# Reordering the first and last areas of an attention stage, its variance step, and the routing statistics of a mixture of experts

## The chip, the core and the metric

The kernel runs on one core of a Trainium2 chip. The metric is the device time of one execution in microseconds (us). The core has a tensor engine (PE, with its weight loads shown as PEld), a vector engine (DVE), a scalar engine (ACT), a general engine (POOL) and a queue engine for transfers (SP). Each executes its own instructions in the order in which the program gives them, and waits for the others by semaphores.

## The reference, cut to what matters

The input `x` has 2 images of 256 channels and 64 x 64 positions. Two layers follow each other; each adds a mixer and then a feed-forward part to `x`. The change touches the mixer of the first layer and the routing of the feed-forward part of the second.

```
x = x + area_attention(layernorm_over_channels(x))       # layer 0, mixer
t = t + lstm_like_recurrence(layernorm(t))               # layer 0, feed-forward
x = x + convs_and_mamba(layernorm_over_channels(x))      # layer 1, mixer
t = t + experts(layernorm(t))                            # layer 1, feed-forward
```

Area attention cuts the 4096 positions of each image into 4 areas of 1024. In every area and for each of 8 heads of 32 channels it computes `softmax(q k^T / sqrt(32)) v`, where q, k and v are products of the normalised input with weights, scaled and shifted per channel. A 5 x 5 convolution of v per channel (25 taps, over the borders of areas) is added, the sum is projected, and the result is added to `x`.

The experts' layer normalises 8192 tokens of 256 values, computes 8 logits for each, takes the two largest of the softmax, and adds the outputs of those two experts with their weights.

## The kernel before, in words

**Stages.** `body` calls `area_attention` (8 areas), then a recurrence and a second mixer, which together take the middle of the time, then `experts`. The last addition of attention to `x` (L345) is followed at once by the first transposes of the recurrence (L693), which read all of `x`. In `experts`, `route` calls `normalise`, then builds tables of indices, and `run_blocks` computes the experts' blocks.

**The attention loop.** Two groups of 4 heads (c = 0, 1) for each of 8 areas make 16 groups G, each with 16 steps t; one step handles 512 queries (n = t // 8) against 128 keys (m = t % 8). The loop at L555 does the following in each step, and the order of the instructions is the order written there (`manual_schedule`):

- `scores`: 4 small products that place the row maxima (L352), 4 that compute k q (L357), into two PSUM tiles of two banks; ACT takes the exponential of each (L364) into the tiles `ex`. There are three such PSUM tiles, `wide()`, for scores and maxima together, handed out in turn.
- `values` of the step before (L370, into `av_o`).
- small things at the time: `place` (L294 to L301) turns the negated maxima of a half group to rows, which ACT copies (L298) and SP sends to the tile `mx`.
- `maxima` for a coming group: 4 products into two `wide()` tiles (L270) and two reductions on DVE (L275). A group needs 16 of them before its own steps; a table (`AHEAD`) says which step computes which.
- on POOL one addition of two `ex` tiles (L577), from which the softmax sums are made. It is made to wait for the last product of this step's `maxima` and for the last marked DVE operation before it, so that it runs while DVE reduces.
- some taps of the convolution on DVE (L324; the first of each c is L313), as many as the table `TAPS` says.
- tables `MINE`, `SMALL`, `LATE`, `AROUND`, `LATE_AROUND` list further work by step: `query` and `key` (two products each at L166 and an ACT copy at L247), `v_half` (L166, L223), `v_tokens` (L239, L240), `mean` and `variance` (products with a constant matrix at L178, ACT copy at L179), `output` (L166, L339), `sums` (L370 into `po`, then L393, or the DVE chain L397 to L405), and on DVE `centre` (L187), `root` (transpose L199, power on POOL L202 and L203, transpose L206), `scale` (L212), `add_taps` (L332) and `residual` (L345). These products use one PSUM bank, `bank()`, of which there is one buffer.

The odd `ex` tiles have one buffer each, the even ones three: the exponentials of an odd step can only be written when POOL has added those of the odd step before.

**The start.** Before the loop, area 0 is normalised in two halves, by the generator `norm`, whose yields let other work be put between; then q and k of the first half are made and the first 8 maxima of group 0 run. A second set of tables with names in `_FIRST` holds for both groups of area 0: group 0 has two maxima in most of its steps, since its own second 8 and the 16 of group 1 are still missing.

**The end.** After the last step come the last sums, the addition of the taps (L332), the output products (L166) of both channel halves, and the two residuals (L345).

**normalise in experts.** For g = 0 to 15, PE turns 4 tiles of 128 tokens (L1730) and ACT copies them (L1731). Statistics are taken by DVE (L1736, one instruction for 128 values of 128 tokens) for groups 0 to 7 at g = 4 and 8 to 15 at g = 5; `root_in` (L1742 to L1747) and `root_out` (a square root on ACT at L1751, L1752, L1753) make the scale. The products with the centred gate weights (L1774, `gates`), a DVE copy (`take_gates`, L1782), transposes and a copy (`turn_gates`, L1788, L1789) give the logits in four parts; `choose` (L1830 to L1844, run once for each half) finds the two experts; `scale` (L1760 on POOL, L1764 on ACT) writes the normalised rows to DRAM by SP (L1767). After `choose` of the second half follow L1888 and a chain of DVE steps down to the indices (L1944), the fetch of the first weights (L1861) and 16 rounds that build the tables (L1954 to L1966), then the first gather of rows.

Of the kernel before, what the change touches and what calls it, by code (L numbers as in the profile page):

```python
# [18 lines left out]
P = 128  # L19
# [74 lines left out]
def area_attention(tc, sh, ap):  # L94
# [13 lines left out]
    with ExitStack() as ctx:  # L108
# [133 lines left out]
        def rows_of(wt, G, half, name, s, t):  # L242
            A, c = GROUPS[G]
            ps = bank()
            project(wt, c, columns(xns[A]), half, ps)
            out = p2.tile([P, 512], F32, name=f"{name}{half}")
            nc.scalar.activation(out, ps, AF.Identity, scale=s[:, c : c + 1], bias=t[:, c : c + 1])  # L247
            return out

        def query(G, half):  # L250
            if half == 0:
                nms[G] = p3.tile([P, NQ, GH, NM], F32, name="nm")
            qs[G, half] = rows_of(w["wq"], G, half, "q", s_qk, t_qk)

        def key(G, half):
            ks[G, half] = rows_of(w["wk"], G, half, "k", s_qk[:, 2:4], t_qk[:, 2:4])
# [152 lines left out]
        with ExitStack() as own:  # L409
# [10 lines left out]
            def norm(at, half):  # L420
# [6 lines left out]
                root(0, 0, at)  # L427
                root(0, 1, at)
                yield
# [7 lines left out]
            next(second)  # L437
            for _ in first:
                pass
            query(0, 0)  # L440
            key(0, 0)
# [4 lines left out]
            next(second)  # L446
            maxima(0, 2)
            key(0, 1)
            maxima(0, 3)
# [9 lines left out]
            for at, works in enumerate([  # L459
                [(0, 0), (0, 1)], [(1, 0)], [(1, 1)], [],  # L460
            ]):
                maxima(0, at + 4)
                for c, half in works:
                    v_half(0, c, half)
            join(0, 0, nc.vector)
            place(0, 0)
            for half in range(2):
                v_tokens(0, 0, half)
# [11 lines left out]
                2: [(0, v_tokens, 1, 0)], 3: [(0, v_tokens, 1, 1)], 4: [(-1, output, 0, 0)],  # L480
                6: [(1, variance, 0)], 7: [(1, variance, 1)], 8: [(-1, output, 0, 1)],
# [11 lines left out]
                3: [(1, square, 1)], 7: [(1, root, 0)],  # L493
# [5 lines left out]
        FIRST = [  # L499
            {  # L500
                0: [(0, query, 1)], 1: [(1, query, 0)], 2: [(1, key, 0)], 3: [(1, key, 1)],
                4: [(1, query, 1)], 14: [(2, query, 0)], 15: [(2, key, 0)],
            },
            {0: [(1, key, 1)], 2: [(1, query, 1)], 11: [(2, query, 0)], 12: [(2, key, 0)], 15: [(2, key, 1)]},
        ]
        SMALL_FIRST = [{5: [(0, place, 1)], 13: [(1, place, 0)]}, SMALL]
        LATE_FIRST = [{4: [(0, join, 1)], 9: [(1, join, 0)], 13: [(1, join, 1)]}, LATE]
        AROUND_FIRST = [
            {
                6: [(1, mean, 0)], 7: [(1, mean, 1)], 8: [(0, v_tokens, 1, 0)], 10: [(1, variance, 0)],  # L510
                11: [(1, variance, 1)], 12: [(0, v_tokens, 1, 1)],
            },
            {
                1: [(1, v_half, 0, 0)], 3: [(1, v_half, 1, 0)], 4: [(1, v_half, 0, 1)], 6: [(1, v_half, 1, 1)],
                7: [(1, v_tokens, 0, 0)], 8: [(1, v_tokens, 0, 1)], 10: [(2, mean, 0)], 14: [(2, mean, 1)],
            },
        ]
        LATE_AROUND_FIRST = [
            {
                7: [(1, centre, 0)], 8: [(1, centre, 1), (1, square, 0)], 9: [(1, square, 1)],  # L520
                11: [(1, root, 0)], 12: [(1, root, 1), (1, scale, 0)], 13: [(1, scale, 1)],
            },
            LATE_AROUND[1],
        ]
# [4 lines left out]
        AHEAD_FIRST = [{}, {**AHEAD, 0: [(1, 0), (1, 1)], 1: [(1, 2), (1, 3)]}]  # L529
        for t in range(1, 14):  # L530
            AHEAD_FIRST[0][t] = [order.pop(0) for _ in range(2 if t < 12 else 1)]

# [5 lines left out]
            [3] + [0] * 11 + [2, 2, 4, 4],  # L538
            [1, 1, 3, 2, 2, 2, 3, 2, 2, 2, 2, 3, 3, 2, 3, 2],
# [15 lines left out]
        for g in range(16 * len(GROUPS)):  # L555
# [3 lines left out]
            new = A == 0  # L559
# [5 lines left out]
            works(G, t, SMALL_FIRST[c] if new else SMALL, {})  # L565

            mm, before = None, latest[0]
            for k, at in (AHEAD_FIRST[c] if new else AHEAD).get(t, ()):
# [12 lines left out]
            for _ in range((TAPS_FIRST if new else TAPS)[c][t]):  # L581
                next(conv, None)
            works(G, t, FIRST[c] if new else MINE, (AROUND_FIRST if new else AROUND)[c])
            if g in due:
                sums(*due.pop(g))
            works(G, t, LATE_FIRST[c] if new else LATE, (LATE_AROUND_FIRST if new else LATE_AROUND)[c])
# [6 lines left out]
            else:  # L593
                pairs = (pairs if m % 4 else []) + [exs]
        nc.gpsimd.tensor_tensor(pairs[-1][1], pairs[-1][1], odd, ALU.add)
        values(*pending)
        for g in sorted(due):
            sums(*due[g])
        last = len(AREAS) - 1
        add_taps(last, 1)  # L600
        for co in range(2):
            for half in range(2):
                output(last, co, half)
            residual(last, co)
# [1014 lines left out]
def experts(tc, sh, ap, out, half, left):  # L1619
# [19 lines left out]
    with ExitStack() as ctx:  # L1639
# [64 lines left out]
        def normalise(p2, logits, halves):  # L1704


            with ExitStack() as own:
# [89 lines left out]
                for g in range(TILES // K):  # L1797
# [9 lines left out]
                    if g == 5:  # L1807
                        for i in range(8, TILES // K):
                            measure(i)
                        root_in()  # L1810
                    if 4 < g < 12 and g % 4 == 2:
                        turn_gates(*waiting)
                    if g == 10:
# [449 lines left out]
```

## Time and profile before

| | us |
|---|---|
| median of 3 runs (3035.07 to 3035.3) | 3035.14 |
| the profiled execution itself | 3031.56 |
| its span, first to last instruction | 3029.7 |
| attention's first step begins (first L352) | 69.85 |
| second group of area 0 begins | 184.2 |
| area 1 begins | 290.2 |
| areas 2 to 6 begin | 467.9, 643.8, 818.7, 994.1, 1170.9 |
| last step's exponentials (L364) begin | 1492.1 |
| last residual of attention ends | 1530.97 |
| first transposes of the experts' normalise | 2324.17 |
| first table step (L1954) | 2384.96 |
| first gather of rows | 2424.6 |

Over the span PE is busy for 90%, DVE 72%, ACT 44%, POOL 45%. A timeline row reads: start, duration, engine, line, operation, output and input with shapes, count, and in brackets the idle time before it and what ended that. A wait row reads: who waited for whom, total, times, longest. A window row gives the busy time of each engine in a stretch, with the number of instructions, and the clock that PE was granted as a share of full speed.

### The profile page before, as it was taken

How to read it: one execution, taken by the hardware profiler on the slowest of the kernel's cores; microseconds unless marked ns; L12 is line 12 of the kernel's file. 1: busy time of each engine (PE TensorE's matmuls, PEld its weight loads, DVE VectorE, ACT ScalarE, POOL GpSimd, SP SyncE). 2: the span in 40 equal slices, each digit the busy share in tenths (PEclk: the TensorE clock that was granted, in tenths of full speed). 3: DMA queues.
4: the chain of work that ended last, by engine and by line, in shares of the span. 5: the costliest groups of instructions: out<-in, count | busy, mean ns of one | idle time of the engine just before them, and what ended most of it. 6: DMA issues, size and time to landing. Idle time of an engine off the chain costs nothing. (4 is left out here: it accounts for less than half of the span.)

```text
span 3029.7 us, 45443 instructions
## 1 busy us (share of the span) xinstructions
PE 2738.2 (90%) x17798; PEld 1519.2 (50%) x17798; DVE 2181.1 (72%) x3224; ACT 1347.7 (44%) x2417; POOL 1358.4 (45%) x1037
## 2 busy tenths in 40 slices
PE   6989999999999999998789999978887589999994
PEld 2222232332323233222179999963444478888882
DVE  4689999999989999898956676679988812222115
ACT  2334454554544454444444455557653822222223
POOL 1354545544454554545623000028773156666651
PEclk8999999999999999999889999989999789999995
DMA  3000000000000000000024000005552446666658
GB/s 126 1 1 1 1 1 1 1 1 1 1 1 1 1 1 1 2 1 1 5 87 161 2 1 1 2 12 153 146 145 64 159 164 228 227 226 227 227 189 337
DMA packets 58658, 220.33 MB, mean 73 GB/s; under 512 B 14440, under 2 KB 15344, under 8 KB 48704
## 3 DMA queue, kind: packets, MB, share of 16 engines
q0 software_dynamic: 25440, 125.24, 11.6%
q1 hardware_dynamic: 31760, 87.82, 9.0%
q10 hardware_dynamic: 1232, 4.25, 0.4%
q8 instruction: 142, 2.33, 0.3%
q14 instruction: 84, 0.69, 0.1%
HBM read 173.30 MB, written 43.58 MB: 72 GB/s over the span
## 5 line engine op out<-in xcount | busy, mean ns | idle before, releaser
L577 POOL TENSOR_TENSOR ex<-ex,ex 128x1024 f32<-128x1024 f32 x255 | 614.5, 2412 | 645.3 <-PE ps L270 287.5
L275 DVE TENSOR_REDUCE nm<-ps 128x2 f32<-128x1024 f32 x512 | 601.0, 1218 | 102.4 <-PE ps L270 101.6
L364 ACT ACTIVATE ex<-ps 128x1024 f32<-128x1024 f32 x512 | 497.9, 1022 | 308.2 <-PE ps L357 269.3
L324 DVE SCALAR_TENSOR_TENSOR acc<-vh,w_pe,acc 128x1008 f32<-128x1008 f32 (+7 forms) x384 | 553.0, 1442 | 7.1
L270 PE MATMUL ps<-k,q 32*128 32x512 f32 x2048 | 347.7, 644 | 13.1 <-DVE nm L275 13.1
L2007 DVE COPY xt<-px 128x512 f32<-128x512 f32 x68 | 47.0, 691 | 397.7 <-PE px L2005 397.7
L2019 ACT ACTIVATE act<-ph,wt 128x256 f32<-128x256 f32 x272 | 128.8, 474 | 396.0 <-PE ph L2017 391.9
L2017 PE MATMUL ph<-xt,wt 128*128 128x256 f32 x1088 | 293.2, 393 | 3.3 <-ACT act L2019 1.7
L357 PE MATMUL ps<-q,k 32*128 32x512 f32 x2048 | 285.0, 607 | 0.0
L370 PE MATMUL av_o<-ex,vt 128*32 128x512 f32 x2048 | 278.0, 609 | 4.8 <-ACT ex L364 4.6
L2027 PE MATMUL py<-wt,act 128*128 128x256 f32 x1088 | 279.6, 380 | 0.0
L270 PEld LDWEIGHTS ps<-k,q 32*128 32x128 f32 x2048 | 123.1, 184 | 216.1 <-issue 75.0
L2017 PEld LDWEIGHTS ph<-xt,wt 128*128 128x128 f32 x1088 | 191.6, 192 | 66.4 <-DVE xt L2007 23.4
L774 PE MATMUL z<-xs,u 128*128 128x128 f32 x1872 | 222.2, 275 | 0.4 <-ACT xs L754 0.4
L774 PEld LDWEIGHTS z<-xs,u 128*128 128x128 f32 x1872 | 215.7, 192 | 0.6 <-ACT xs L754 0.6
L2027 PEld LDWEIGHTS py<-wt,act 128*128 128x128 f32 x1088 | 202.2, 191 | 25.0
L798 ACT ACTIVATE t<-z,bias 128x128 f32<-128x128 f32 x468 | 136.3, 361 | 144.5 <-PE z L786 144.4
L2042 POOL DMA_INDIRECT results<-y,ri x136 | 138.0, 1015 | 139.4 <-DVE y L2035 98.3
L786 PE MATMUL z<-xs,v 128*128 128x128 f32 x1512 | 180.1, 275 | 0.1
L786 PEld LDWEIGHTS z<-xs,v 128*128 128x128 f32 x1512 | 174.3, 192 | 0.7 <-DVE xs L805 0.7
L1508 POOL TENSOR_TENSOR cs<-hs,cs 128x1024 f32<-128x1024 f32 x63 | 148.7, 2363 | 54.1 <-DVE hs L1501 32.7
L370 PE MATMUL po<-ex,ones 128*32 128x512 f32 x1024 | 136.6, 638 | 37.0 <-ACT rows L298 25.7
(408 smaller groups left out, 3809.9 us busy)
## 6 DMA issues: line engine op xcount, KB each, us to landing
cs<-c_rows SPq DMA_DIRECT2D x128, 256.0 KB
y<-results SPq DMA_DIRECT2D x32, 512.0 KB
x<-xrows SPq DMA_DIRECT2D x8, 1024.0 KB
rows<-xt SPq DMA_DIRECT2D x16, 512.0 KB
out_x<-res POOLq DMA_DIRECT2D x15, 512.0 KB, 7.1
xrows<-xn SPq DMA_DIRECT2D x24, 256.0 KB
x<-in_x SPq DMA_DIRECT2D x4, 1024.0 KB
x<-in_x ACTq DMA_DIRECT2D x4, 1024.0 KB
```

The costliest lines, as they stand in the source:

```text
L270: mm = nc.tensor.matmul(tiles[h // 2][:, h % 2], qs[G, i // HM][head(h), i % HM * P : (i % HM + 1) * P], ks[G, n][head(h)], start=True, st ...
L275: nc.vector.tensor_reduce(nms[G][:, n, 2 * j : 2 * j + 2, i], tiles[j], AX.X, ALU.max, negate=True)
L324: mark(nc.vector.scalar_tensor_tensor(part, vh[:, c, 2 + r0 + dy : 2 + r1 + dy, w0 + dx : w1 + dx], w_pe[:, c, k : k + 1], part, ALU.mult, ...
L357: nc.tensor.matmul(tiles[h // 2][:, h % 2], k[head(h), m % HM * P : (m % HM + 1) * P], qs[G, n][head(h)], start=False, stop=True, tile_pos ...
L364: nc.scalar.activation(exs[i], tiles[i], AF.Exp, scale=HD**-0.5)
L370: nc.tensor.matmul(to[head(h)], lhs, exs[h // 2][:, h % 2], start=first, stop=last, tile_position=(0, HD * h))
L577: add = nc.gpsimd.tensor_tensor(pair[0], *pair, ALU.add)
L774: nc.tensor.matmul(z[c][:, g, :m], u[:, k, c, g], xt[:, k], start=g == GATES[0] and k == 0, stop=False, skip_group_check=True,)
L786: nc.tensor.matmul(z[c][:, g, :m], v[:, k, c, g], h[:, k], start=False, stop=k == 1, skip_group_check=True,)
L1508: nc.gpsimd.tensor_tensor(now["c", n], hs, now["c", n], ALU.mult)
L2017: nc.tensor.matmul(ph[:, hc], wt[:, at : at + P], xt[:, c], start=c == 0, stop=c == 1)
L2027: nc.tensor.matmul(py[:, j], act[:, hc, j * P : j * P + P], wt[:, at : at + C], start=hc == 0, stop=hc == NH - 1,)
```

## The change

The diff has two parts.

In attention:

- `query` and `key` can take a PSUM place from outside. Before the loop, q and k of the first half use `wide()` tiles instead of the single bank; q of the second half of group 0 and q and k of group 1 are made before the loop as well (they were steps 0 to 2 of group 0).
- The two `mean` steps of area 1 are put in before the first half of area 0 is scaled (they were steps 6 and 7 of group 0).
- In `norm`, the yield between the two halves of `root` is moved, so that two maxima can stand between the power on POOL and the DVE transpose that waits for it. The four `v_half` and the two `v_tokens` are spread between the maxima, and the join and place of the first maxima come after them.
- The tables `_FIRST` hold for group 0 alone; group 1 of area 0 uses the ordinary tables, but keeps its own numbers of taps. Group 0 has two maxima in steps 0 to 9 and one after; no taps before step 10.
- In the ordinary tables, `variance` moves from steps 6 and 7 to 4 and 6, the output that was in step 4 to step 7, and the first half of `root` from step 7 to step 6; the second half stays in step 8.
- After the loop the end is done by halves of 512 positions: add the taps of the half, two output products into one `wide()` tile, ACT copies, residuals; the last sums come between the halves.

In `normalise`: statistics for groups 8 to 11 are taken at g = 5, those for 12 to 15 and `root_in` at g = 9; `root_out` and the first `choose` move from g = 10 to 13; all 16 `scale` steps come after the loop, where 5 of them stood in it.

```diff
-            query(0, 0)
-            key(0, 0)
+            for half in range(2):
+                mean(1, half)
+            for _ in first:
+                pass
+            query(0, 0, wide()[:, 0])
+            key(0, 0, wide()[:, 0])
             next(second)
             maxima(0, 0)
             next(second)
             maxima(0, 1)
-            next(second)
             maxima(0, 2)
+            for _ in second:
+                pass
+            maxima(0, 3)
             key(0, 1)
-            maxima(0, 3)
...
+            for at in range(4):
                 maxima(0, at + 4)
+                v_half(0, *divmod(at, 2))
+            for half in range(2):
+                v_tokens(0, 0, half)
+            query(0, 1, wide()[:, 0])
             join(0, 0, nc.vector)
             place(0, 0)
+            query(1, 0, wide()[:, 0])
+            key(1, 0, wide()[:, 0])
...
-                2: [(0, v_tokens, 1, 0)], 3: [(0, v_tokens, 1, 1)], 4: [(-1, output, 0, 0)],
-                6: [(1, variance, 0)], 7: [(1, variance, 1)], 8: [(-1, output, 0, 1)],
+                2: [(0, v_tokens, 1, 0)], 3: [(0, v_tokens, 1, 1)], 4: [(1, variance, 0)],
+                6: [(1, variance, 1)], 7: [(-1, output, 0, 0)], 8: [(-1, output, 0, 1)],
...
-                3: [(1, square, 1)], 7: [(1, root, 0)],
+                3: [(1, square, 1)], 6: [(1, root, 0)],
...
+        FIRST = {
+            0: [(1, key, 1)], 1: [(1, query, 1)], 11: [(2, query, 0)], 12: [(2, key, 0)], 15: [(2, key, 1)],
+        }
...
+        AHEAD_FIRST = dict(AHEAD)
+        for t in range(14):
+            AHEAD_FIRST[t] = [order.pop(0) for _ in range(2 if t < 10 else 1)]
...
         TAPS_FIRST = [
-            [3] + [0] * 11 + [2, 2, 4, 4],
-            [1, 1, 3, 2, 2, 2, 3, 2, 2, 2, 2, 3, 3, 2, 3, 2],
+            [0] * 10 + [1, 2, 3, 2, 3, 2],
+            [2, 0, 2, 2, 3, 3, 3, 2, 2, 0, 3, 3, 3, 3, 3, 3],
         ]
...
+        for half, at in enumerate(HALVES):
+            if half == 1:
+                for g in sorted(due):
+                    sums(*due[g])
+            y = ys[last, 1][:, at]
+            nc.vector.tensor_tensor(y, y, acc[:, at], ALU.add)
+            ps = wide()
+            for co in range(2):
+                project(w["wpr"], co, lambda k: ys[last, k], half, ps[:, co])
...
+                to = area(last)[:, co, at]
+                nc.vector.tensor_tensor(to, to, o, ALU.add)
...
-                    if g == 5:
-                        for i in range(8, TILES // K):
+                    if g in (5, 9):
+                        for i in range(g + 3, g + 7):
                             measure(i)
+                    if g == 9:
                         root_in()
                     if 4 < g < 12 and g % 4 == 2:
                         turn_gates(*waiting)
-                    if g == 10:
+                    if g == 13:
                         root_out()
                         halves[0]()
-                    if g > 10:
-                        scale(g - 11)
                 last = gates(3)
                 turn_gates(*take_gates(*waiting))
                 turn_gates(*take_gates(*last))
-                for g in range(5, TILES // K):
+                for g in range(TILES // K):
                     scale(g)
```

## The prediction

> **What bounds the kernel now.** I first read the busy times by stage, cut at step starts (the first L352 of a step), then the timeline of each stage that the diff touches, then the waits. The middle stages and the experts' blocks are untouched and only start earlier or later: the first transposes after attention begin 0.5 us after its last residual, and the first gather follows 16 table rounds. So the change is worth what it takes off attention's end and off the start of the tables.
>
> Stages (stretch; length; then busy us of PE, PEld, DVE, ACT, POOL; clock):
>
> ```profile
> 71.60:184.20 112.60, 106.30 (x607) 32.96 (x607) 77.46 (x70) 42.21 (x50) 44.78 (x29) 0.96 0.00 1
> 184.20:290.20 106.00, 95.85 (x583) 29.66 (x582) 96.23 (x84) 43.57 (x52) 43.59 (x29) 0.94 0.00 1
> 467.90:643.80 175.90, 170.05 (x1125) 53.40 (x1124) 164.87 (x149) 86.00 (x102) 89.34 (x55) 0.99 0.01 1
> ...
> 1489.80:1531.50 41.70, 23.41 (x66) 6.50 (x62) 24.64 (x31) 6.89 (x10) 8.03 (x6) 0.67 0.03 7
> ```
>
> In an ordinary area (third row) PE is busy 97% and DVE 94%. Area 0 (first two rows) takes 218.6 us where an ordinary one takes 176: its first group is PE's (DVE idles 35 us), its second DVE's. The last 41.7 us are neither's, a chain of waits.
>
> The start:
>
> ```profile
> 22.08 3.75 PE L166 MATMUL po<-xn,wq 128*128 128x512 f32 x4 [6.35 <-issue]
> ...
> 26.70 3.69 PE L166 MATMUL po<-xn,wk 128*128 128x512 f32 x4 [0.87 <-ACT q L247]
> ...
> 31.26 1.98 PE L178 MATMUL po<-sq,mean_w 128*128 128x512 f32 x4 [0.87 <-ACT k L247]
> ...
> 40.82 0.71 DVE L206 STREAM_TRANSPOSE ln_r<-root 128x512 f32<-128x512 f32 x1 [3.49 <-POOL root L203]
> ...
> 73.89 1.94 ACT L364 ACTIVATE ex<-ps 128x1024 f32<-128x1024 f32 x2 [3.35 <-PE ps L357]
> ```
>
> One projection takes 3.7 us after a PE idle of 6.35 us and 1.98 us later; the single bank puts an ACT copy between q and k; DVE stands 3.49 us for POOL's power with maxima behind it.
>
> Step 8 to 9 of an ordinary area (area 2):
>
> ```profile
> 513.23 5.46 POOL L203 TENSOR_TENSOR root<-root,minus_half 128x32 f32<-128x32 f32 x1
> ...
> 518.65 2.34 POOL L577 TENSOR_TENSOR ex<-ex,ex 128x1024 f32<-128x1024 f32 x1
> 518.72 1.25 DVE L206 STREAM_TRANSPOSE ln_r<-root 128x1024 f32<-128x1024 f32 x1 [3.21 <-POOL root L203]
> ...
> 521.03 1.02 ACT L364 ACTIVATE ex<-ps 128x1024 f32<-128x1024 f32 x1 [3.50 <-POOL ex L577]
> ...
> 522.25 3.31 PE L370 MATMUL po<-ex,ones 128*32 128x512 f32 x16 [3.54 <-ACT rows L298]
> ```
>
> Power, POOL's addition, the exponential that needs its buffer, the rows copy behind it on ACT, PE's sums behind that: step 9 takes 10.4 us (515.14 to 525.50) where its neighbours take 5.35.
>
> The end of attention, and the routing:
>
> ```profile
> 1515.97 3.78 PE L166 MATMUL po<-y,wpr 128*128 128x512 f32 x4 [0.87 <-ACT o L339]
> ...
> 1529.75 1.22 DVE L345 TENSOR_TENSOR x<-x,o 128x1024 f32<-128x1024 f32 x1 [7.93 <-ACT o L339]
> ```
>
> ```profile
> 2346.04 0.42 DVE L1747 TENSOR_REDUCE var<-away 128x64 f32<-128x256 f32 x1
> ...
> 2363.29 0.29 DVE L1789 COPY logits<-by_token 128x128 f32<-128x128 f32 x1 [7.05 <-PE by_token L1788]
> ...
> 2365.31 0.57 DVE L1830 TENSOR_TENSOR pr<-logits,inv 128x256 f32<-128x256 f32 x1
> ```
>
> Every output product runs at the slow rate with an ACT copy in between. In the routing DVE idles 7.05 us before the third part of the logits, since the last turns wait on ACT behind scales.
>
> **What the Trainium skill says.** "TensorE: Matmul & The Clock Gate", "What's actually happening": PE runs at half clock by default and at full clock after about 3.4 us of sustained work. The trace agrees: 3.7 against 1.98 us for the same four products. "SBUF — State Buffer", "Who interferes with whom": a DVE instruction with two SBUF inputs and a POOL instruction that reads SBUF exclude each other for a whole instruction. The trace agrees: the L212 pair beside the addition at 518.65 takes 2.08 us for one operation and 1.21 us elsewhere; a tap and an addition issued back to back take turns, 3.3 us a pair (POOL's 16.01 us for 5 additions at 1469.47), against 1.3 for a tap alone.
>
> **Part by part.**
>
> *Start.* The two means of area 1 fill PE from 16.4 to 21.0 (1.98 each plus a 0.58 copy; the x of area 1 has landed by 12.3 us, by its transfer's packets), so the clock stays up: q 22.05 to 24.0, and k at once after it from its own PSUM tile, done on ACT at 26.8 instead of 31.2. First maxima at 27.9 instead of 33.2. Power hidden behind two maxima (4.7 us of DVE against 3.5): k of the second half at ACT by 40.9 instead of 48.8. Then the four rounds of maxima and v at the 2.98 us pace of the old trace, from 42.1 to 53.1; tokens 2.5, q of the second half 2.0, place at 57.9. The rows go out at 58.75; the old trace has 4.6 us from the rows copy to the last L352 (67.02 to 71.62), hence 63.35, and q and k of group 1 (4 us) lie inside that. The loop is entered some 8.3 us earlier with 8 us of PE projections and the means (4 us) already done.
>
> *Group 0.* A step with two maxima and a projection took 7.6 us (100.56 to 108.17), without projection 5.7, with tokens 6.3. New steps 0 to 9: 6.1, 7.6, 6.3, 6.3, 7.6, 7.6, 7.6, 5.7, 5.7, 7.6, sum 68.1; DVE's root, two scales and sums pile up in 7 to 9, +1.5: step 10 at 133. DVE then has, of the 173.7 us that both groups had (77.5 + 96.2), plus 3 for the taps that ran ahead of the loop, minus 4 for taps that stood for POOL around 184, 172.7; some 55 of it done by then (20 maxima at 2.27, 45; centre, transposes, scale, sums, 10). The rest, 117.7 us, is more than PE's (30 for steps 10 to 15, 82 after), so DVE is the bound at its ordinary 96 to 97%: 121.5 us. Area 1 begins at 254.5 to 261 against 290.2; with a little more DVE debt handed on I take **31 us** saved, bounds 22 and 36.
>
> *Variance and root one step earlier* (six areas). POOL's order is now root, addition 7, addition 8. In area 2's times: DVE ends the two taps of step 6 at 508.0, transposes to 509.2; power ends at 515.1, addition 7 at 517.4. The transpose after it no longer waits. But the scale reaches DVE at 517.3, just before addition 8 can start; if it takes its turn first, addition 8 ends at 521.0, as now, and nothing is gained; if POOL wins, it ends at 519.8 and the step is 1.2 us shorter, with a warmer clock 2. Behind DVE's earlier transpose, one reduction is late by 0.65 us, which the later stall covers. I take 0.5 per area, **3 us**; bounds -4 (0.65 uncovered) and +14 (six times 2.3). The output moved to step 7 costs PE the same two products.
>
> *End.* Taps end at 1505.6 and are unchanged. add_taps 1.22, half-add 0.68; two products 3.8 and 2.8 (slow, then warming) to 1513.5; sums 2.0, the DVE chain 3.1 and add 0.7 to 1519.3; remaining products 3.0, copy 0.78, residual 0.68: 1523.8 to 1524.5 against 1530.97. **6.5 us**, bounds 3 (all slow) and 8. The setup of the next stage (1.21 us wait for bc_rest on DVE) falls in gaps.
>
> *Routing.* Two counts of statistics: 16 at 0.193 after the first gates, then DVE waits for the second gates (PE 2340.45) and takes 30 more: to 2347.0. root_in 2.7: 2349.7, that is 3.3 us later than 2346.46. Root and first choose 2.9 + 6.3: 2358.9. Two rounds of copy, transpose, copy: 3.5: second choose at 2362.4 instead of 2365.31. **2.5 us** after a slow-clock allowance; bounds 0 and 4. The 16 scales now lie after the turns: ACT 16 x 1.49 from 2353.5 to 2377.4, before 2378.4, so the exponents behind them are no later; the SP row writes end 40 us before the first gather.
>
> Sum: 31 + 3 + 6.5 + 2.5 = 43. The profiled execution's 3031.56 becomes 2988.6; the median of the runs stands 3.6 us above it, so 2992.
>
> **Rivals.** *A, area 0 gives less*: PE cools between the sparse maxima at 31 to 37 us, and the three-tap steps hold PE through the shared PSUM tiles, as at 184 to 205 (PE idle 8 us). For: DVE has no slack there. Against: additions are tied to reductions. Then 20 instead of 31 and nothing from the root: 3006. *B, POOL wins the race* in the six areas: 11 us more, 2981. *C, slower*: the root in step 6 puts POOL's additions off the reductions, and they stay off, so that taps take turns with them: 2.0 us for each tap met. Area 0's second group (37 taps) and six areas meet them; from about 22 taps on the gain of 43 is eaten, at 4 per area and 8 in area 0 (32 taps, 64 us) it is 3056. Against: by step 10 POOL has 3 us of slack in each step. *D, nothing*: the last PE wait just moves to the area's other stalls, 3033.
>
> **Numbers.** Likeliest case 0.62, own range 2984 to 3002; A 0.18, B 0.15, C 0.03, D 0.02. The bounds of the terms added are -21 and -62 (3014, 2973); all ends do not fall together, and 2978 to 3010 leaves under 2 in 10 out. Faster 0.95, within 0.2% (6 us, about what can be told from no change) 0.02, slower 0.03.
>
> **What would show it.** Start: the first L364 near 64.5, q and k of the first half at 1.98 us. Area 0: area 1 begins near 258, DVE over 95% busy in its second group. Root: no wait of L206 for L203, yet ACT's wait for POOL's L577 stays once in each area. End: last L345 18.5 us after the last tap. Routing: L1747 later, L1954 earlier by 2 to 3 us. I am wrong if area 1 begins after 270, or if step 9 still costs as much while something else in an ordinary area grows.

## The result, and the profile after

The changed kernel takes 3003.18 us (median of 3 runs, 3001.11 to 3006.58) against 3035.14: a ratio of 0.990, 95% interval 0.9886 to 0.9914. It is faster by 32 us; forecast were 43 (2992, range 2978 to 3010). The time lies inside that range, but 1 us outside the range given for the likeliest case (2984 to 3002), and nearer to the 3006 of rival A than to 2992.

The profiled execution of after is the one of 3003.18 us, span 3001.4, so between the two profiles the gain is 28.3 us. The rest of the 32 is that the profiled execution of before lay 3.6 us under its median and that of after on it. Read by stage, from marks in the two timelines (the forecast of the first row is the prediction's for the entry of the loop; its own mark for the first exponential, 64.5 us, would be 9.4):

| stage ends at | before | after | gain in the stage | forecast |
|---|---|---|---|---|
| first exponential (L364) | 73.89 | 65.60 | 8.3 | 8.3 |
| area 1 begins (first L352) | 290.2 | 266.1 | 15.8 | 22.7 |
| last tap of attention ends | 1505.67 | 1477.27 | 4.3 | 3 |
| first transposes of the recurrence | 1531.51 | 1505.57 | -2.5 | 6.5 |
| first transposes of normalise | 2324.17 | 2298.12 | 0.1 | 0 |
| second choose begins | 2365.31 | 2336.85 | 2.4 | 2.5 |
| first gather of rows | 2424.58 | 2396.35 | -0.2 | 0 |
| end of the span | 3029.7 | 3001.4 | 0.1 | 0 |

Two stages carry nearly the whole error: area 0 gave 7 us less, and the end lost 2.5 where 6.5 were to be gained.

The stages again as windows (stretch; length; busy us of PE, PEld, DVE, ACT, POOL; clock), cut at the same places as before: group 0 and group 1 of area 0, and the end.

```profile
64.30:175.20 110.90, 103.74 (x607) 31.84 (x607) 84.87 (x76) 41.31 (x48) 43.79 (x31) 0.94 0.00 1
175.20:266.10 90.90, 84.87 (x561) 26.13 (x561) 88.17 (x80) 41.43 (x49) 40.78 (x26) 0.98 0.00 1
...
1461.40:1505.60 44.20, 19.40 (x71) 5.59 (x71) 26.25 (x33) 7.79 (x10) 10.56 (x15) 0.73 0.05 12
```

Group 1 is DVE's to 97%, as forecast, and 15 us shorter. Group 0 is only 1.7 us shorter than the 112.6 of before. Three projections (6 us of PE) and two means (4 us) left it, but PE's busy time fell only from 106.3 to 103.7 us: one projection (k of area 1's first group), a `v_half` and two more rounds of maxima came in, and part of the rest ran at the lower clock (0.94 against 0.96). The last stretch, which was to shrink, is longer.

The start in the timeline of after:

```profile
22.23 1.98 PE L166 MATMUL ps<-xn,wq 128*128 128x512 f32 x4 [0.99 <-DVE xn L212]
24.05 1.88 PE L166 MATMUL ps<-xn,wk 128*128 128x512 f32 x4
...
36.15 0.69 DVE L206 STREAM_TRANSPOSE ln_r<-root 128x512 f32<-128x512 f32 x1
...
65.60 1.94 ACT L364 ACTIVATE ex<-ps 128x1024 f32<-128x1024 f32 x2 [1.99 <-PE ps L357]
```

q and k follow each other at 1.98 and 1.88 us, no idle time stands before the transpose L206, and the first exponential begins 1.1 us after the forecast 64.5.

Step 8 to 9 of area 2 (POOL's additions are L564 here):

```profile
488.50 5.46 POOL L203 TENSOR_TENSOR root<-root,minus_half 128x32 f32<-128x32 f32 x1
...
493.93 7.96 POOL L564 TENSOR_TENSOR ex<-ex,ex 128x1024 f32<-128x1024 f32 x3
...
494.79 1.24 DVE L206 STREAM_TRANSPOSE ln_r<-root 128x1024 f32<-128x1024 f32 x1
...
496.06 1.31 DVE L212 TENSOR_TENSOR xn<-xn,ln_r 128x1024 f32<-128x1024 f32 x1
...
499.60 1.02 ACT L364 ACTIVATE ex<-ps 128x1024 f32<-128x1024 f32 x1 [2.26 <-POOL ex L564]
...
500.82 2.49 PE L370 MATMUL po<-ex,ones 128*32 128x512 f32 x16 [2.29 <-ACT rows L298]
```

The scale in before, where POOL's addition had begun first:

```profile
520.00 2.08 DVE L212 TENSOR_TENSOR xn<-xn,ln_r 128x1024 f32<-128x1024 f32 x1
```

DVE no longer waits for the power; ACT still waits for POOL's addition, 2.26 us instead of 3.50, and PE behind it 2.29 instead of 3.54. That is what was to be seen. In the race between DVE's scale and POOL's second addition DVE has the first turn, in all six areas: the scale takes 1.31 us instead of 2.08, and the addition 3.32 instead of 2.34. Counted from the start of step 7 that addition ends only 0.3 us sooner than in before (16.3 against 16.6 us in area 2).

The end:

```profile
1492.79 3.78 PE L166 MATMUL ps<-y,wpr 128*128 128x512 f32 x4 [0.87 <-ACT o_last L597]
...
1497.42 0.69 DVE L601 TENSOR_TENSOR x<-x,o_last 128x512 f32<-128x512 f32 x1 [3.96 <-ACT o_last L597]
...
1498.41 0.65 POOL L1119 DMA_DIRECT2D bc_rest<-in_b_conv  x1 [27.97 <-DVE bc_parts L628]
...
1504.42 0.76 PE L1116 MATMUL w_dt<-w_dtp,w_xdt 4*128 4x128 f32 x2 [7.85 <-DMA w_dtp<-in_w_dtp]
...
1505.57 4.75 PE L690 MATMUL turned<-ident,x 128*128 128x128 f32 x24 [0.38 <-DVE w_dt L1117]
```

The last residual (L601) ends 20.8 us after the last tap, against 25.3 before. But the transfers of the next stage's setup are only issued after it, and its product w_dt waits for them on PE, ahead of the first transposes. In before they were issued at 1505.8 to 1506.6, 24 to 25 us before the last residual ended, and the transposes followed that residual by 0.5 us. Now they follow it by 7.5. Before:

```profile
1505.81 0.36 SPq L1107 DMA_DIRECT2D taps<-in_c_rows  x1
...
1506.27 0.65 POOL L1122 DMA_DIRECT2D bc_rest<-in_b_conv  x1 [7.42 <-issue]
```

The routing, on DVE:

```profile
2323.41 0.42 DVE L1744 TENSOR_REDUCE var<-away 128x64 f32<-128x256 f32 x1
...
2336.52 0.29 DVE L1786 COPY logits<-by_token 128x128 f32<-128x128 f32 x1 [1.27 <-PE by_token L1785]
2336.85 0.42 DVE L1826 TENSOR_TENSOR pr<-logits,inv 128x256 f32<-128x256 f32 x1
```

Counted from normalise's first transposes the variance is ready 3.4 us later (forecast 3.3) and the second choose starts 2.4 us sooner (2.5); the idle 7.05 us is gone.

### The profile page after: what moved, and what is told of

It is laid out like the page before. It is cut to its first block, busy times and chain, and to the rows that moved or that the text cites. A ratio compares the mean times of both kernels' runs of the same rounds, so it can differ in the third digit from the quotient of the medians.

```text
span 3001.4 us, 45442 instructions
## 1 busy us (share of the span) xinstructions
PE 2724.7 (91%) x17798; PEld 1512.9 (50%) x17798; DVE 2173.2 (72%) x3227; ACT 1348.5 (45%) x2417; POOL 1358.1 (45%) x1037
## 5 line engine op out<-in xcount | busy, mean ns | idle before, releaser
L564 POOL TENSOR_TENSOR ex<-ex,ex 128x1024 f32<-128x1024 f32 x255 | 617.3, 2425 | 615.1 <-PE ps L270 248.9
L364 ACT ACTIVATE ex<-ps 128x1024 f32<-128x1024 f32 x512 | 498.0, 1022 | 318.2 <-PE ps L357 285.5
L370 PE MATMUL av_o<-ex,vt 128*32 128x512 f32 x2048 | 280.8, 615 | 4.8 <-ACT ex L364 4.6
L352 PE MATMUL ps<-mx,ones_b 3*128 3x512 bf16 x1024 | 132.4, 386 | 37.2 <-DVE nm L275 35.0
```

Source lines behind the costliest of these rows:

```text
L364: nc.scalar.activation(exs[i], tiles[i], AF.Exp, scale=HD**-0.5)
L370: nc.tensor.matmul(to[head(h)], lhs, exs[h // 2][:, h % 2], start=first, stop=last, tile_position=(0, HD * h))
L564: add = nc.gpsimd.tensor_tensor(pair[0], *pair, ALU.add)
```

## The experiments

In the experiments the executions of one kernel, before included, spread over 4 to 17 us, much of it in stages that nobody edited (from the first transposes of the recurrence to those of normalise: 789.5 to 800.7 us in the 14 profiles). So small effects are read from the profile of each kernel, by stage, and the times stand beside them. Each stage is then one execution of one kernel; where several kernels share a stage, their spread is given. Ratios are to the kernel before on the same chip; they lie up to 0.0012 from the quotients of the medians beside them.

| kernel | median us | before beside it | ratio, 95% interval |
|---|---|---|---|
| routing alone | 3037.02 | 3038.72 | 0.9993 (0.9984 to 1.0001) |
| end alone | 3041.28 | 3038.72 | 1.0003 (0.9992 to 1.0014) |
| after, o_last elsewhere | 3006.94 | 3038.72 | 0.9884 (0.9865 to 0.9902) |
| after, root back | 3018.62 | 3038.72 | 0.9931 (0.9916 to 0.9947) |
| after, four steps filled | 3003.68 | 3032.85 | 0.9907 (0.9893 to 0.9922) |
| after, o_last elsewhere, two tiles | 2990.63 | 3032.85 | 0.9856 (0.9838 to 0.9874) |
| after, scale later | 3000.29 | 3032.85 | 0.9906 (0.9888 to 0.9925) |
| these edits together | 2995.89 | 3032.85 | 0.9868 (0.9851 to 0.9885) |
| two tiles, two steps filled | 2992.45 | 3032.92 | 0.9862 (0.9845 to 0.9879) |
| area 0 alone | 3011.96 | 3032.92 | 0.9933 (0.9915 to 0.9952) |
| two tiles, taps early | 2980.85 | 3032.92 | 0.9824 (0.9810 to 0.9838) |
| the same, PE warmed at the start | 2987.96 | 3038.02 | 0.9837 (0.9814 to 0.9860) |

The theory that the experiments test: the parts add up; the end lost because the setup of the next stage came to wait for the new tiles `o_last`; group 0 lost because PE's clock falls in the steps that the change emptied. The rivals stand in the expectations.

### Parts alone: routing, end, area 0; and the root taken back

The routing alone, on the kernel before:

```diff
-                    if g == 5:
-                        for i in range(8, TILES // K):
+                    if g in (5, 9):
+                        for i in range(g + 3, g + 7):
...
-                    if g == 10:
+                    if g == 13:
...
-                    if g > 10:
-                        scale(g - 11)
```

> The kernel before with the routing part of the change alone. Theory (the prediction's term): the second choose starts 2.4 us sooner after the first transposes of normalise, the table rounds follow without change: 3032.7 against 3035.1. Rival: the 16 scales behind the turns hold up the exponents or the gathers, so that the 2.4 us are given back before the first gather: 3035.

From the first transposes of normalise to the second choose: 38.68 us, 41.14 before, so 2.46 us; from there to the first gather 59.1 against 59.3, so the rival (the gain is given back) falls. Over all 14 profiles the first stretch takes 41.1 to 41.9 us in the three with the old routing and 38.7 to 39.4 in the eleven with the new. The term stands. In the time it is too small to be told from nothing (the interval holds 1).

The end alone, on the kernel before:

```diff
-        add_taps(last, 1)
-        for co in range(2):
-            for half in range(2):
-                output(last, co, half)
-            residual(last, co)
+        for half, at in enumerate(HALVES):
...
+            ps = wide()
```

> The kernel before with the end by halves alone. Theory: the last residual ends 4 to 5 us sooner after the last tap, but the next stage's setup (bc_parts, bc_rest, taps, w_dtp) starts only after it, since o_last lies where the setup's tiles come, and the first transposes begin 2 to 3 us later than before: 3037.6, slower. Rival (the prediction): the setup falls in gaps and 6.5 us are gained: 3028.6.

From the last tap to the last residual 23.1 us (25.3), from there to the first transposes 7.1 (0.5): together 30.2 against 25.8. The residual came 2.2 us sooner, not 4 to 5, and the loss is 4.3, not 2 to 3. The setup's transfer bc_rest is issued 0.3 us after the last residual here too. Over all profiles the old end takes 24.1 to 25.8 us from tap to transposes, the new one as written 28.2 to 30.6. The time itself can't tell 2.5 us slower from none (interval 0.9992 to 1.0014), but it excludes the 6.5 us of the prediction (0.9979).

The start and the tables of area 0 alone, on the kernel before (start, `FIRST` tables and taps of the diff above):

> The kernel before with the start and the tables of area 0 alone; ordinary areas, end and routing as before. Theory (parts add up): first exponential 3 to 8 us sooner, area 0 about 203 us instead of 218.9, area 1 some 3 us longer: 18 to 21 us in all, 3012 to 3015 when before is at 3033. Rival: the parts hang together (the root in step 6 was needed for area 1), and area 0 alone gives less than 12 us: over 3021.

21 us by the medians (3011.96 against 3032.92). First exponential at 65.1, area 0 202.0 us, area 1 180.5: the parts add up.

The root taken back, on the changed kernel:

```diff
-                2: [(0, v_tokens, 1, 0)], 3: [(0, v_tokens, 1, 1)], 4: [(1, variance, 0)],
-                6: [(1, variance, 1)], 7: [(-1, output, 0, 0)], 8: [(-1, output, 0, 1)],
+                2: [(0, v_tokens, 1, 0)], 3: [(0, v_tokens, 1, 1)], 4: [(-1, output, 0, 0)],
+                6: [(1, variance, 0)], 7: [(1, variance, 1)], 8: [(-1, output, 0, 1)],
...
-                3: [(1, square, 1)], 6: [(1, root, 0)],
+                3: [(1, square, 1)], 7: [(1, root, 0)],
```

> The changed kernel with variance, root and output in their old steps in the ordinary areas, group 0 of area 0 as changed. Theory: step 9 of areas 1 to 6 is 0.5 to 1 us longer each, 3 to 6 us in all: 3007. Rival 1 (the addition on POOL had been won): about 11 us longer, 3014. Rival 2: the areas differ only by what is handed on from area 0, nothing from the root: 3003.

Areas 2 to 6 take 175.61 us each, as in before (175.70), and 174.55 in after: the move is worth 1.1 us an area. Its place: steps 7 to 10, counted from exponential to exponential, take 26.91 us together with the root back, 26.94 in before, 25.88 in after. In the other kernels that have the move they take 25.3 to 26.1, so it is worth 0.8 to 1.6 us. POOL did not win the race (that was 2.3 an area in the prediction), and the move is not worth nothing. Most of the 1.1 us is PE's clock. The sums of step 9 (L370 into `po`) begin 0.3 us sooner with the move, counted from the start of step 7 and in each of the areas 2 to 6 (0.5 in area 4). Then they take 1.92 us, or 2.5 to 3.6 where the clock has fallen. In the five kernels with the old places they take 1.92 in 3 of 25 areas, in the seven with the new places and the old scale in 19 of 35. PE waits 3.54 us ahead of them in area 2 of before and 2.29 in that of after; that the shorter wait keeps the clock up fits this, but no run tests it. The edit takes back three moves, of variance, root and output, and no run separates the output's part.

By the time this kernel stands 9 us above after (0.9931 against 0.990), which is near rival 1's 11. The profiles don't bear that out: of the 13.2 us between the two spans, 5.1 stand ahead of the first exponential and 2.6 behind attention, where the edit changes nothing; areas 2 to 6 and the last one together account for 7.3.

### The end: where o_last lies, and its PSUM tile

```diff
-                o = p2.tile([P, 512], F32, name="o_last", tag=f"q{half}")
+                o = p3.tile([P, NA], F32, name="o_last", tag="tmp")[:, :512]
```

Only the place of the copies in SBUF changes. If the setup's tiles (bc_parts, bc_rest, taps, w_dtp) lie where `o_last` was, they now need not wait for it.

> The changed kernel with the copies o_last in tiles of another pool. Theory: the setup's DMAs are issued before the residuals again, near 1479, and the first transposes follow the last residual within 1 us instead of 7.5: 6 to 7 us less than the changed kernel, near 2996.5. Rival: the setup's instructions then stand between the residuals on DVE and PE, or the wait is the DMAs' own time wherever it lies: 3003, no change.

```profile
1482.77 0.65 POOL L1119 DMA_DIRECT2D bc_rest<-in_b_conv  x1 [7.43 <-issue]
...
1497.61 3.78 PE L166 MATMUL ps<-y,wpr 128*128 128x512 f32 x4 [0.87 <-ACT o_last L597]
...
1502.24 0.69 DVE L601 TENSOR_TENSOR x<-x,o_last 128x512 f32<-128x512 f32 x1 [3.96 <-ACT o_last L597]
...
1503.48 2.86 PE L690 MATMUL turned<-ident,x 128*128 128x128 f32 x12 [0.44 <-DVE w_dt L1117]
```

The transfer goes out 20 us before the last residual, the transposes follow that residual by 0.55 us, and from the last tap to the transposes it is 21.3 us instead of 28.3. The 7.0 us are the place of a tile, since nothing else was edited. That the setup's first instructions wait for what last used their memory fits this, but the traces hold no addresses; what they show is that in after POOL's bc_rest waits for DVE, until the last residual has read `o_last`, and that without the shared place the setup stands ahead of the residuals also in the order of DVE's instructions. The rival falls: the setup's small steps on DVE now run in the wait for ACT. The time doesn't show the 7 us: expected was 2996.5, measured 3006.94, at a ratio (0.9884) hardly under that of after (0.990). This profile is also 5.0 us longer before the first exponential and 4.9 us longer between the first transposes of the recurrence and those of normalise, neither of which was edited.

The PE line shows what is left: 0.87 us of waiting for ACT, although the product writes the other half of the PSUM tile than ACT reads, and then the slow rate.

```diff
-            ps = wide()
             for co in range(2):
-                project(w["wpr"], co, lambda k: ys[last, k], half, ps[:, co])
+                ps = wide()[:, 0]
+                project(w["wpr"], co, lambda k: ys[last, k], half, ps)
```

> The changed kernel with o_last elsewhere as in the run before, and with a PSUM tile for each of the four output products of the end instead of one tile for two. Theory: a product no longer waits 0.87 us for ACT's copy of the other half of its tile, and the last one follows its neighbour at once and at full clock (2.0 instead of 3.78 us): from the last tap to the first transposes 3 to 4 us less than the 21.3 us with o_last elsewhere alone. Rival: the wait is only handed on to ACT and the residuals on DVE, 1 us or less.

```profile
1494.79 2.84 PE L166 MATMUL ps<-y,wpr 128*128 128x512 f32 x6 [3.07 <-DVE y L592]
...
1498.48 0.69 DVE L601 TENSOR_TENSOR x<-x,o_last 128x512 f32<-128x512 f32 x1 [1.02 <-ACT o_last L597]
...
1499.43 2.94 PE L690 MATMUL turned<-ident,x 128*128 128x128 f32 x14 [0.44 <-DVE w_dt L1117]
```

17.1 us from the last tap to the transposes, 4.2 less: the wait of 0.87 us is gone, and the last two products run on at full clock in one piece. The second part is not certain in each execution: of the five kernels with this end, three take 17.1 us and two (all together, warm start) 19.3 and 19.8, since their last products ran slow. So the two tiles are worth 1.5 to 4.2 us, and the idea of halves 4 to 9 us against the old end's 24.1 to 25.8, once both of its waits are gone.

### Group 0: the clock and the pile-up

Three stretches of 3.41 us in after, in steps 4, 7 and 8 of group 0:

```profile
92.69:96.10 3.41, 3.41 (x20) 0.57 (x16) 0.65 (x2) 2.26 (x3) 1.48 (x5) 0.54 0.00 0
119.97:123.38 3.41, 2.53 (x12) 0.57 (x11) 3.41 (x4) 0.00 (x0) 3.41 (x1) 0.97 0.00 0
123.38:126.79 3.41, 3.39 (x18) 0.94 (x17) 3.29 (x2) 1.26 (x2) 3.36 (x2) 0.50 0.02 5
```

The clock (the third number from the end) halves in or right after steps that hold no projection (2, 3, 7, 8), while DVE reduces. The test adds one that nothing reads:

```diff
+        def fill(G):
+            project(w["wq"], 0, lambda k: area(0)[:, k], 0, bank())
+
         FIRST = {
-            0: [(1, key, 1)], 1: [(1, query, 1)], 11:...
+            0: [(1, key, 1)], 1: [(1, query, 1)], 2: [(0, fill)], 3: [(0, fill)], 7: [(0, fill)], 8: [(0, fill)], 11:...
```

> The changed kernel with one more projection (4 products, read by nothing) in each of steps 2, 3, 7 and 8 of group 0, where the change left PE without one. Theory: PE's clock falls there for want of work (0.54 at 92.7 to 96.1 us, 0.50 to 0.53 between 123.4 and 137), so with 8 us of work added the clock stays at 1.00, steps 4, 8 and 9 take 7.6 instead of 8.8, 9.7 and 8.6 (from exponential to exponential), group 0 takes 3 to 6 us less than 111.5, and area 1 begins that much sooner. Rival 1: DVE's pile-up (root, join, scale) sets those steps; then group 0 takes 111.5 or up to 6 us more. Rival 2: DVE is the bound of group 1, and what group 0 gains, group 1 loses: 0 for area 0 as a whole.

The same stretches of this kernel's profile:

```profile
92.69:96.10 3.41, 3.35 (x24) 1.34 (x26) 2.02 (x3) 1.21 (x2) 2.85 (x5) 1.00 0.00 0
119.97:123.38 3.41, 3.25 (x16) 1.08 (x16) 2.31 (x3) 1.05 (x2) 3.33 (x2) 1.00 0.02 5
```

The clock stays up and steps 8 and 9 take 7.7 us each, so the falls do come from want of work. But steps 2 and 3 now take 8.6 and 8.3 (6.8 and 7.4 in after), group 0 in all 112.1 (112.5 in after), area 0 204.1. The expected gain did not come; the numbers are those of the rivals.

> The kernel with o_last elsewhere and two tiles, with the unread projection in steps 7 and 8 of group 0 alone (the four fills before cost steps 2 and 3 some 2.5 us, which is what they gave back). Theory: steps 8 and 9 take 7.7 us each and the clock stays at 1.00 from 123 us on; group 0 takes 108 to 109.5 us instead of 111.5, area 1 begins 2 to 3.5 us sooner after the first exponential. Rival: the falls merely move to steps 3 and 4, or to steps 10 and 11, and group 0 stays at 111.

Steps 8 and 9 take 7.7 us, but group 0 takes 111.0, the rival's number, and a fall comes in group 1 instead (clock 0.66 from 216 to 226 us), which takes 93.3; area 0 204.3. So filling, in these two forms, is no remedy. What the falls cost shows where an execution was spared them by chance: group 0 has the same instructions in the same order in five more of the kernels, and its first ten steps, 79.8 us in after, take 78.2 and 79.8 with o_last elsewhere (one tile and two), 75.3 in two kernels (area 0 alone, root back) and 73.7 in the one with the later scale, whose clock is 1.00 from 64 to 144 us:

```profile
64.00:94.00 30.00, 27.70 (x160) 9.09 (x162) 20.40 (x18) 12.32 (x15) 5.86 (x3) 1.00 0.00 1
94.00:125.00 31.00, 29.23 (x183) 8.85 (x185) 21.08 (x20) 10.68 (x14) 15.19 (x11) 1.00 0.01 2
125.00:144.00 19.00, 15.41 (x107) 4.33 (x100) 18.73 (x18) 6.25 (x8) 8.39 (x8) 1.00 0.00 1
```

At the end of area 0 less of this is left: it takes 203.3 us in after, 202.0 in the two kernels with 75.3, and 199.1 with the later scale.

### DVE as the bound of group 1

```diff
-            [0] * 10 + [1, 2, 3, 2, 3, 2],
-            [2, 0, 2, 2, 3, 3, 3, 2, 2, 0, 3, 3, 3, 3, 3, 3],
+            [1] * 6 + [0] * 4 + [1, 2, 3, 2, 3, 2],
+            [2, 0, 2, 2, 3, 2, 2, 2, 2, 0, 3, 2, 3, 2, 2, 2],
```

> The kernel with o_last elsewhere and two tiles, with six of the 37 taps of group 1 of area 0 moved into steps 0 to 5 of group 0, where DVE idles about 3 us a step while it waits for maxima. Theory: DVE bounds group 1 and the handing-on to area 1, so 6 taps of 1.3 us less there take 6 to 8 us off group 1 and the first two steps of area 1 (91.9 + 14.3), while group 0 gains at most 2: 4 to 7 us less in all. Rival: PE bounds group 1 as it does an ordinary area (88), or the taps delay the maxima of group 0 by what they take: within 2 us of the kernel without the move.

Group 1, first the kernel with two tiles, then this one:

```profile
180.45:271.29 90.84, 84.82 (x559) 26.13 (x558) 88.11 (x80) 41.47 (x49) 40.77 (x26) 0.98 0.00 1
```

```profile
173.02:259.76 86.74, 84.20 (x559) 26.01 (x559) 84.00 (x77) 41.23 (x49) 42.05 (x27) 0.98 0.00 1
```

Group 1 is 4.1 us shorter with the same PE work, the first two steps of area 1 take 11.4 instead of 16.0, and group 0, which took the six taps, is not longer (110.8 against 112.5). The kernel with two tiles had falls of the clock in group 0, which this execution did not have. Area 0 alone is the fairer neighbour, as its first ten steps took the same 75.3 us: there group 0 takes 110.8 as well, group 1 91.3 and the two steps 14.4. Against it the six taps are worth 7.5 us, within the 6 to 8 of the theory for these two stretches, and group 0 pays nothing. The mechanism was right; the 4 to 7 in all were a little low. With 2980.85 us (2979.75 to 2983.45) it is the best of all kernels here, 1.76% (1.62 to 1.90) below before.

### POOL's race, all together, and a warm start

```diff
-                8: [(1, root, 1), (1, scale, 0)], 9: [(-1, residual, 0)], 10: [(1, scale, 1)],
+                8: [(1, root, 1)], 9: [(-1, residual, 0), (1, scale, 0)], 10: [(1, scale, 1)],
```

> The changed kernel with the scale of the first channel half moved from step 8 to step 9 in the ordinary areas, so that DVE does not take turns with POOL's addition there. Theory: the second addition of step 8 ends 1 us sooner, step 9 is about 1 us shorter in each of six areas: 5 to 7 us. Rival: the scale then meets the addition of step 9 or delays the reductions or the rows, and the six areas stay at 174.6 us each.

The rival (no gain over the six areas) holds: POOL's addition of step 8 falls from 3.32 to 2.35 us, as intended, and step 9 from 8.6 to 7.0, but step 10, which now holds the scale's work, rises from 5.6 to 6.75, and an area takes 174.1 where others with the old place take 174.0 to 174.8. What the scale took is not gone but one step on.

> The changed kernel with the four edits together: o_last elsewhere, two tiles, filled steps and the later scale. Theory: the gains add up, 7 + 3.5 + 4 + 5, near 20 us less than the changed kernel: 2983 to 2986. Rival: only the end's two count, 10 us: 2993.

2995.89 is near the rival's 2993: the fills and the later scale add nothing to the two edits of the end, as their own runs had it. Here the last output products ran slow, so that the end took 19.3 us instead of 17.1.

The last kernel is the one with the early taps, with this before the first mean:

```diff
+            warm = bank()
+            for i in range(24):
+                nc.tensor.matmul(warm[:, :P], sh.mean_w, sh.mean_w, start=True, stop=True)
```

> The kernel of the run with six taps moved, with 24 products of the constant matrix with itself (128 x 128, read by nothing) on PE ahead of the first mean, while x is on its way. Theory: the start comes in two lengths (first exponential at 65 or at 70.7 us in the profiles so far) because the clock rises between the first and the third product of the start, by chance of its phase; with PE at work before x lands the first product takes 1.98 instead of 3.75 us, and the first exponential begins at 62 to 64 us: 1.5 to 3 us below the 65.1 of that run, 2 to 5 less in the median than 2980.9. Rival: x lands too late or the clock is down again by then, and the start stays at 65 or 70.7: 2981.

First lines of PE: this kernel, then the one without the products, then the one with o_last elsewhere.

```profile
1.06 7.85 PE L413 MATMUL po<-mean_w 128*128 128x128 f32 x48 [1.06 <-DVE eps L74]
8.97 1.98 PE L178 MATMUL po<-x,mean_w 128*128 128x512 f32 x4
```

```profile
6.16 3.74 PE L178 MATMUL po<-x,mean_w 128*128 128x512 f32 x4 [6.16 <-DMA x<-in_x]
10.57 1.98 PE L178 MATMUL po<-x,mean_w 128*128 128x512 f32 x4 [0.68 <-ACT pm L179]
```

```profile
6.17 3.75 PE L178 MATMUL po<-x,mean_w 128*128 128x512 f32 x4 [6.17 <-DVE qk_s L87]
10.60 3.78 PE L178 MATMUL po<-x,mean_w 128*128 128x512 f32 x4 [0.68 <-ACT pm L179]
```

The clock part of the theory is right as far as the first products go: warmed, each of them takes 1.98 us. The kernel is no better (2987.96; the intervals of the two ratios overlap). The 7.85 us of products overran the arrival of x at 6.2 by 2.8 us, so that the second product comes 1.1 us later than without them (11.63 in this kernel); the products between 38 and 48 us ran slow for 2 us more, and the first exponential came at 68.2 instead of 65.1. By their mean rate about 15 products would have ended in time (an estimate from the 7.85 us for 24); that was not tried. The second and third fence are two executions of the same start: whether the second product is slow differs between executions of the same instructions, and over all ten profiles of this start the first exponential comes at 64.9 to 67.4 or at 69.6 to 70.9 us.

## Why the prediction was right in its range, and wrong in two of its sums

- **Start: right within 1.1 us, in part by luck.** The entry of the loop was forecast at 63.35 and came at 64.3, the first exponential at 64.5 and came at 65.6. The luck is that the start of these instructions varies by 5 us between executions (65 to 71), and the profiled one was of the short kind. Where the forecast was too early, twelve products of maxima at 32.89 took 4.34 us and the projection behind them 3.70: rival A's cooling, where A put it, but at 1 us. The "8 us of PE projections" done ahead of the loop are 6: three projections moved.
- **Group 0: wrong.** "New steps 0 to 9 ... sum 68.1; ... pile up in 7 to 9, +1.5: step 10 at 133." From the entry at 64.3 to step 10 at 142.5 it was 78.2 us, where 69.6 were forecast. Of the 8.6 us too many, 4.5 to 6.1 are falls of the clock (79.8 against 75.3 and 73.7 for the same ten steps, first L352 to first L352), in or right after the steps from which the change took the projections; the rest, 2.5 to 4.1, are step times from before's warm steps, applied to steps that also hold a join, a root or transposes (6.7, 7.0, 7.8 us for steps 7 to 9 without a fall, where I had 5.7, 5.7 and 7.6, and 1.5 for the pile-up). Removing 2 us of PE work from a step was counted as a gain of up to 1.9 us; it took away what kept the clock up. Not all of the falls reach area 1: area 0 is 1.3 to 4.3 us shorter where the execution was spared them.
- **Group 1: right.** From step 10 to area 1 121.5 us were forecast at DVE's rate; it was 123.5, DVE 97% busy, and moving six taps off it took 4.1 to 4.5 us off the group.
- **Handing on: seen, too small.** The "little more DVE debt" cost 3.2 us in area 1 (180.9 against 177.7), so that 20.9 us of the 31 were left at area 2. That is rival A's number, but only in part by A's road: A saw the clock fall in the start, where it cost 1 us, and not in group 0.
- **Root: waits as forecast, size low.** 3 us for six areas; measured 1.1 an area, 5.8 over areas 2 to 6, with the output's move in it. The wait of L206 went and ACT's stayed, but shorter by 1.24 us, and PE's sums behind it were quicker (2.49 instead of 3.31). DVE's scale did take its turn first, and "nothing is gained" was nearly so for the addition, which ended 0.3 us sooner; the rest came from sums at full clock (19 of 35 areas, 3 of 25 in the old places), the "warmer clock" that I had granted only if POOL won. The output moved to step 7, which I priced at nothing, took 1.7 us off the last area, which has no root (157.5 to 155.8 from its first exponential to the last tap; 157.8 with it back).
- **End: wrong.** "6.5 us ... The setup of the next stage (1.21 us wait for bc_rest on DVE) falls in gaps." It no longer starts before the last residual: 7.0 us, shown by moving o_last alone. I had taken the overlap in before's trace as given and not asked what memory allowed it. A further 2.3 us is the residual coming 20.8 us after the last tap instead of 18.5: the last product waited 0.87 us for its PSUM tile and then ran slow (3.78 us). With two tiles it was 16.8 in three profiles, and 19.1 and 19.5 in the two where the last products ran slow.
- **Routing: right**, the two marks of the forecast (variance 3.3 us later, second choose 2.5 sooner) within 0.1 us.
- **The sum.** 43 forecast, 28.3 between the profiles: -7 in area 0, -9 in the end, +1.3 in the areas between (5.8 and 1.7 less the 3.2 handed on, where 3 stood). The median hid 3.6 of that, by the offset between before's profile and its median, which I carried over and which after did not have. That the time fell into the stated range at all, with two of the four parts wrong, owes to the range being wide.

## What to carry to other kernels

Taking work off an engine that paces its own clock is only a gain if what is left keeps it busy; price such a step at both clocks. When a stage's last tiles are renamed or moved, look at which tiles of the next stage will lie in their memory, since its first transfers wait for them, and read the overlap that the old trace shows as something that can be lost. And where one engine bounds the second half of a stage and idles in the first, move its work forward before shortening the first half: six taps moved were worth 7.5 us, while emptying the steps of group 0 shortened it by 1.9.

## What the runs showed of the hardware

- The Trainium skill ("TensorE: Matmul & The Clock Gate", "What's actually happening") has the clock back at half after an idle window of about 3.4 us, the windows running freely. Here it fell to 0.50 after a stretch (119.97 to 123.38 us) in which PE counts as busy for 2.53 of 3.41 us and no wait of its rows is longer than 0.74 us, so no idle window was needed. Most of the products in it use 32 rows; with one projection of 128 rows more in the step the clock stayed at 1.00. Which of the two counts, rows or busy time, no run separates. Windows that run freely would fit the start, which differs by 5 us between executions of the same instructions; no run shows their phase.
- A product into one half of a two-bank PSUM tile waited 0.87 us for ACT's copy of the other half, both times, until the halves were two tiles; in these runs the wait goes with the tile of the program, not with the half that is used.
- A scale on DVE with two SBUF inputs and an addition on POOL lengthen each other by who begins first: in each of six areas of after DVE began first, and the scale took 1.31 us and the addition 3.32; with the root back POOL began first, and they took 2.08 and 2.34; with the scale moved away they took 1.22 and 2.35.
